# A recommender's lookups and layers: features transposed tile by tile, layers in blocks of two tiles, tables split by TensorE

## The chip, the cores and the metric

The kernel runs on one core of a Trainium2 chip. The metric is the device time of one execution in microseconds, the median of several runs. A profile is one execution recorded by the hardware's profiler, with all engines: TensorE (PE, its weight loads apart as PEld), VectorE (DVE), ScalarE (ACT), GpSimd (POOL) and the DMA queues.

## What is computed

For each of 16384 samples: 32 word rows of 300 floats are gathered from a table of 50000 rows and averaged; three bags of 20 rows of 64 floats are averaged from small tables (1000, 5000 and 10000 rows); four single rows come from tables of 100, 50, 20 and 1000 rows. The 748 features go through three layers. A scalar per looked-up row of the small tables (`wide`) is summed and added at the end.

```python
tok = word_emb[token_idx].mean(axis=1)            # 32 rows of 300
e1 = emb_mh1[mh1_idx].mean(axis=1)                # 20 rows of 64, and e2, e3 alike
o1 = emb_oh1[oh1_idx]                             # and o2, o3, o4
emb = jnp.concatenate([tok, e1, e2, e3, o1, o2, o3, o4], axis=1)   # 748
wide = (wide_mh1[mh1_idx].sum(axis=(1, 2)) + ... + wide_oh4[oh4_idx][:, 0])[:, None]
h = jax.nn.relu(emb @ W1 + b1)                    # 1024
h = jax.nn.relu(h @ W2 + b2)                      # 512
h = jax.nn.relu(h @ W3 + b3)                      # 256
return jax.nn.sigmoid(h @ Wd + bd + wide)
```

## The kernel before

A tile is 128 samples, and there are 128 tiles. Two things go on side by side.

The word rows are gathered by GpSimd: one indirect DMA per token position brings 128 rows of 1200 bytes, 32 of them per tile. VectorE adds them up.

```python
for q in range(n_groups):                          # 16 groups of two gathers
    rows = tokp.tile([P, TOK_GROUP * TOK_D], F32, name="tok_rows")     # 6 buffers
    for r in range(TOK_GROUP):
        nc.gpsimd.indirect_dma_start(
            out=rows[:, r * TOK_D : (r + 1) * TOK_D], out_offset=None, in_=word,
            in_offset=bass.IndirectOffsetOnAxis(ap=it[:, j : j + 1], axis=0))
    under_way.append((t, q, rows))
    if len(under_way) > TOK_LAG:                   # three groups later
        add_up(*under_way.pop(0))                  # two tensor_add on VectorE
```

The small tables are not gathered. Their rows lie on the chip, cut into 138 slices of 128 rows. VectorE makes one-hot rows for the slice number and for the row in the slice (`row`, `slice`), TensorE multiplies them into counts (`pc`), ScalarE copies the counts out (`cnt`, 8 bits), and TensorE multiplies the counts with the tables (`pg`). So that this is exact enough in 16 bits, each fp32 table is held as three bf16 terms, made once at the start:

```python
for part in range(n_h // PART):                    # six parts of 23 slices
    ...
    for c in range(3):
        if c:
            nc.vector.scalar_tensor_tensor(
                rows, rows, 2.0 if c == 1 else 1.0, term[c - 1], op0=ALU.mult, op1=ALU.subtract)
        nc.scalar.activation(term[c], rows, AF.Copy, scale=2.0 if c == 0 else 1.0)
        yield 1
```

The counts of a tile are made in 11 steps of 6 sample pairs. The program writes into each step the one-hots of the next step, this step's counts, some gathers, some of the last tile's sums, and some of the layers. The layers are fp32 and run over blocks of four tiles (512 columns), after a transpose of the block's features; the last tiles form blocks of two, one and one.

```python
def transposed(x, gs):                             # once per block of four tiles
    for k in range(NK):                            # six chunks of features
        pt = ps_h.tile([P, BLOCK], F32, name="pt", tag="ph")
        for s, g in enumerate(gs):
            nc.tensor.transpose(pt[:kk, s * P : (s + 1) * P], chunk(g, k), ident)
        nc.vector.tensor_scalar(x[:kk, k, 0:n], pt[:kk, 0:n], scale[:kk, k : k + 1], None, ALU.mult)
        yield CHUNK_WORK

def layer(dst, weights, bias, src, kks, n_out, n):
    for m in range(n_out):
        ph = ps_h.tile([P, BLOCK], F32, name="ph", tag="ph")           # two buffers in PSUM
        for k, kk in enumerate(kks):
            nc.tensor.matmul(ph[:, 0:n], weights[:kk, k, m * P : (m + 1) * P], src[:kk, k, 0:n],
                             start=(k == 0), stop=(k == len(kks) - 1))
            ...
        nc.scalar.activation(dst[:, m, 0:n], ph[:, 0:n], AF.Relu, bias=bias[:, m : m + 1])
```

The steps are put in order like this (cut):

```python
sizes = [NSUB] * (tiles // NSUB - 1) + [NSUB - 2, 1, 1]                # blocks of tiles
for t in range(tiles + 1):
    ...
    for i in range(STEPS):
        if t < tiles:
            hot = one_hots(sc, s, i + 1)
            counts(cnt, hot_now, i)
            tables_on_chip.to(TABLE_PACE * (t * STEPS + i - 2))
            toks.to(n_groups * (i + 1) / STEPS)
        done = next(sums) if sums else 0
        if layers:
            share = (n_h + layers_time) * (i + 1) / STEPS - done
            layers.to((layers_before + share) / LAYER_TIME)
    ...
    if len(gs) == sizes[0]:
        layers = Paced(mlp(b0, gs, wides))
```

Of the kernel before, what the change touches and what calls it, by code (L numbers as in the profile page):

```python
# [17 lines left out]
P = 128  # L18
# [5 lines left out]
TOK_LAG = 3  # L24
BLOCK = 512
HALF = P // 2
N_SMALL = 3 * N_MH + 4
ONEHOT = 6
STEPS = -(-HALF // ONEHOT)
CHUNK_WORK = 1  # L30
TABLE_PACE = 1.2
LAYER_TIME = 10
# [6 lines left out]
G_COLS = TOK_D + 7 * ROW  # L39
# [7 lines left out]
def kernel(  # L47
# [23 lines left out]
    NSUB = BLOCK // P  # L71
# [5 lines left out]
    for f in SMALL:  # L77
# [4 lines left out]
    tokp = ctx.enter_context(tc.tile_pool(name="tok", bufs=2 * TOK_LAG))  # L82
    const = ctx.enter_context(tc.tile_pool(name="const", bufs=1))
    idxp = ctx.enter_context(tc.tile_pool(name="idx", bufs=2))
# [4 lines left out]
    gp = ctx.enter_context(tc.tile_pool(name="g", bufs=NSUB + 1))  # L89
    wp = ctx.enter_context(tc.tile_pool(name="wide", bufs=2 * NSUB))  # L90
    xp = ctx.enter_context(tc.tile_pool(name="x", bufs=1))
# [8 lines left out]
        [(0, 128)],  # L100
        [(128, 256)],
        [(256, 300), (684, 748)],
        [(300, 428)],
        [(428, 556)],
        [(556, 684)],
    ]
# [7 lines left out]
    scale = const.tile([P, NK], F32, name="scale")  # L114
    nc.vector.memset(scale, 1.0)
    nc.vector.memset(scale[:, 0:2], 1.0 / N_TOK)
    nc.vector.memset(scale[0 : TOK_D - 256, 2:3], 1.0 / N_TOK)
    nc.vector.memset(scale[:, 3:4], 1.0 / N_MH)
    nc.vector.memset(scale[0:EMB, 4:5], 1.0 / N_MH)
# [23 lines left out]
    PART = n_h // 6  # L143

    def load_tables(part0, tag):
        raw = xp.tile([P, PART, ROW], F32, name="raw", tag=tag)
        for f in SMALL:
            table, (h0, h1) = tables[f], slices[f]
            full, rest = divmod(table.shape[0], P)
            a, b = max(h0, part0), min(h0 + full, part0 + PART)  # L150
            if a < b:
                nc.sync.dma_start(
                    out=raw[:, a - part0 : b - part0, :],
                    in_=table[(a - h0) * P : (b - h0) * P, :].rearrange("(h p) d -> p h d", p=P),
                )
            if rest and part0 <= h0 + full < part0 + PART:
                nc.vector.memset(raw[:, h0 + full - part0, :], 0.0)
                nc.sync.dma_start(out=raw[0:rest, h0 + full - part0, :], in_=table[full * P :, :])
        return raw

    def convert_tables():
# [3 lines left out]
        raws = [load_tables(k * PART, tags[k]) for k in range(2)]  # L165
        yield
        for part in range(n_h // PART):
            rows = raws[part]
            if 1 <= part < n_h // PART - 1:
                raws.append(load_tables((part + 1) * PART, tags[(part + 1) % 2]))  # L170
            for c in range(3):
                term = [
                    terms[:, part * PART : (part + 1) * PART, k * ROW : (k + 1) * ROW]
                    for k in range(3)
                ]
                if c:
                    nc.vector.scalar_tensor_tensor(
                        rows, rows, 2.0 if c == 1 else 1.0, term[c - 1], op0=ALU.mult, op1=ALU.subtract
                    )
                nc.scalar.activation(term[c], rows, AF.Copy, scale=2.0 if c == 0 else 1.0)  # L180
                yield 1
# [22 lines left out]
    under_way = []  # L204
    features = {}

    def add_up(t, q, rows):
# [4 lines left out]
        else:  # L212
            nc.vector.tensor_add(tok_sum, tok_sum, a)  # L213
            to = features[t][:, 0:TOK_D] if q == n_groups - 1 else tok_sum
            nc.vector.tensor_add(to, tok_sum, b)  # L215

    def tokens(t, it):


        for q in range(n_groups):  # L220
            rows = tokp.tile([P, TOK_GROUP * TOK_D], F32, name="tok_rows")
            for r in range(TOK_GROUP):
                j = q * TOK_GROUP + r
                nc.gpsimd.indirect_dma_start(  # L224
                    out=rows[:, r * TOK_D : (r + 1) * TOK_D],
                    out_offset=None,
                    in_=word,
                    in_offset=bass.IndirectOffsetOnAxis(ap=it[:, j : j + 1], axis=0),
                )
            under_way.append((t, q, rows))  # L230
            if len(under_way) > TOK_LAG:
                add_up(*under_way.pop(0))
            yield 1

    def last_tokens():
        for group in under_way:
            add_up(*group)

    def load_indices(blk):
# [15 lines left out]
        return it, ix  # L255
# [71 lines left out]
    def small_sums(g, cnt):  # L327
# [3 lines left out]
        for i in (0, 2, 4, 6):  # L331
# [9 lines left out]
            at = TOK_D + i * ROW  # L341
# [9 lines left out]
    def wide_term(g):  # L351
        wide = wp.tile([P, 1], F32, name="wide")
        at = TOK_D + EMB
        nc.vector.tensor_reduce(
            wide,
            g[:, at : at + 6 * ROW].rearrange("p (c d) -> p c d", d=2 * ROW)[:, :, 0:2],
# [3 lines left out]
        nc.vector.tensor_add(wide, wide, g[:, G_COLS - 1 : G_COLS])  # L360
        return wide

    def chunk(g, k):
        if k < 2:
            return g[:, k * P : (k + 1) * P]
        if k == 2:
            return g[:, 2 * P : TOK_D + EMB]
        at = TOK_D + (1 + 2 * (k - 3)) * ROW + 1
        return g[:, at : at + 2 * EMB]

    def transposed(x, gs):

        n = len(gs) * P
        for k in range(NK):
            kk = chunk_k[k]
            pt = ps_h.tile([P, BLOCK], F32, name="pt", tag="ph")
            for s, g in enumerate(gs):
                nc.tensor.transpose(pt[:kk, s * P : (s + 1) * P], chunk(g, k), ident)  # L378
            nc.vector.tensor_scalar(  # L379
                x[:kk, k, 0:n], pt[:kk, 0:n], scale[:kk, k : k + 1], None, ALU.mult  # L380
            )
            yield CHUNK_WORK

    def layer(dst, weights, bias, src, kks, n_out, n):
        for m in range(n_out):
            ph = ps_h.tile([P, BLOCK], F32, name="ph", tag="ph")
            for k, kk in enumerate(kks):
                nc.tensor.matmul(  # L388
                    ph[:, 0:n],
                    weights[:kk, k, m * P : (m + 1) * P],  # L390
                    src[:kk, k, 0:n],
                    start=(k == 0),
                    stop=(k == len(kks) - 1),
                )
                if k < len(kks) - 1:
                    yield 1
            nc.scalar.activation(dst[:, m, 0:n], ph[:, 0:n], AF.Relu, bias=bias[:, m : m + 1])  # L397
            yield 1

    def mlp(b0, gs, wides):  # L400

        n = len(wides) * P
        x = xp.tile([P, NK, BLOCK], F32, name="x", tag="even")
        yield from transposed(x, gs)
        h1 = xp.tile([P, M1, BLOCK], F32, name="h1", tag="odd")
        yield from layer(h1, w1_sb, b1_sb, x, chunk_k, M1, n)
        h2 = xp.tile([P, M2, BLOCK], F32, name="h2", tag="even")
        yield from layer(h2, w2_sb, b2_sb, h1, [P] * M1, M2, n)
        h3 = xp.tile([P, M3 + 1, BLOCK], F32, name="h3", tag="odd")
        yield from layer(h3, w3_sb, b3_sb, h2, [P] * M2, M3, n)  # L410
        po = ps_h.tile([1, BLOCK], F32, name="po", tag="ph")
        for k in range(M3):
            nc.tensor.matmul(  # L413
                po[:, 0:n], wd_sb[:, k : k + 1], h3[:, k, 0:n], start=(k == 0), stop=False
            )
        for s, wide in enumerate(wides):
            nc.tensor.matmul(  # L417
                po[:, s * P : (s + 1) * P], wide, ident, start=False, stop=(s == len(wides) - 1)
            )
        y = h3[0:1, M3, 0:n]  # L420
        nc.scalar.activation(y, po[:, 0:n], AF.Sigmoid, bias=bd_sb)
# [3 lines left out]
    class Paced:  # L425


        def __init__(self, gen):
            self.gen, self.done = gen, 0

        def to(self, size):
            while self.done < size:
                work = next(self.gen, None)
                if work is None:
                    return
                self.done += work
# [27 lines left out]

    tiles = B // P
    mlp_time = (NK * (CHUNK_WORK + M1) + M1 * M2 + M2 * M3 + M3) * LAYER_TIME
    ctx.enter_context(tc.manual_schedule())
    sizes = [NSUB] * (tiles // NSUB - 1) + [NSUB - 2, 1, 1]
    it, ix = load_indices(0)
# [5 lines left out]
    gs, wides, layers, before, b0 = [], [], None, None, 0  # L475
    for t in range(tiles + 1):
        s = t % NSUB
        sums = None
        if before:
            features[t - 1] = g = gp.tile([P, G_COLS], F32, name="g")  # L480
            sums = sums_by_step(small_sums(g, before))
        if t < tiles:
            if s == 0 and t:
                it, sc = next_it, next_sc
            cnt = cp.tile([P, 2, HALF, n_h], FP8, name="cnt", tag="counts")
            toks = Paced(tokens(t, it[:, s, :].bitcast(U32)))
        else:
            last_tokens()
        for i in range(STEPS):
            if t < tiles:  # L490
                hot_now = hot
                if s == 1 and i == 0 and t + NSUB < tiles:
                    next_it, ix = load_indices(t // NSUB + 1)
                if s == 2 and i == 0 and t + NSUB < tiles + 1:
                    next_keys = lookup_keys(ix)
                if i < STEPS - 1:
                    hot = one_hots(sc, s, i + 1)
                elif t + 1 < tiles:
                    hot = one_hots(next_sc if s == NSUB - 1 else sc, (s + 1) % NSUB, 0)
# [65 lines left out]
```

## Time and profile before

| what | value |
|---|---|
| time, median of 3 runs | 7126.95 us (7116.23 to 7129.94) |
| span of the profiled execution | 5269.3 us |
| mean granted TensorE clock in it | 0.989 |
| gathers (GpSimd) | 4096, 951 ns each |
| TensorE matmuls in the record | 41320 |
| layer matmuls in the record (two per fp32 matmul) | 5984, busy 1474.1 + 1211.0 us |
| sums from the tables, `pg` | 17664, busy 1849.6 us |
| counts, `pc` | 16384, busy 758.4 us |
| one-hots on VectorE | 2816, busy 762.4 + 797.9 us |
| token adds on VectorE | 3968, 479 ns each |
| HBM traffic | 123 GB/s |

The profiled execution is shorter than the measured ones; the table gives both. In the lines of the profile, a group of instructions stands with its count, its busy time, the mean length of one, and the idle time of its engine before it with what ended that idle time. Matmuls overlap in a pipeline, so the mean length of one is longer than the busy time divided by the count. A weight load (PEld) runs beside the matmul ahead of it.

### The profile page before, as it was taken

How to read it: one execution, taken by the hardware profiler on the slowest of the kernel's cores; microseconds unless marked ns; L12 is line 12 of the kernel's file. 1: busy time of each engine (PE TensorE's matmuls, PEld its weight loads, DVE VectorE, ACT ScalarE, POOL GpSimd, SP SyncE). 2: the span in 40 equal slices, each digit the busy share in tenths (PEclk: the TensorE clock that was granted, in tenths of full speed). 3: DMA queues.
4: the chain of work that ended last, by engine and by line, in shares of the span. 5: the costliest groups of instructions: out<-in, count | busy, mean ns of one | idle time of the engine just before them, and what ended most of it. 6: DMA issues, size and time to landing. Idle time of an engine off the chain costs nothing.

```text
span 5269.3 us, 104252 instructions
## 1 busy us (share of the span) xinstructions
PE 5094.7 (97%) x41320; PEld 3164.7 (60%) x41320; DVE 3768.8 (72%) x8014; ACT 2447.1 (46%) x1938; POOL 3897.3 (74%) x4103
## 2 busy tenths in 40 slices
PE   4799999999999999999999999999999999999999
PEld 3565656566565656656655656556566566656658
DVE  8777777777777777777777777777777777777752
ACT  5444444444444444444444444444444444444432
POOL 7777777777777777777777777777777777777762
PEclk8899999999999999999999999999999999999999
DMA  6444444444444444444444444444444444444431
GB/s 190 125 125 124 125 125 126 126 125 124 125 125 125 125 124 125 125 125 126 125 124 125 126 125 126 124 125 125 125 125 125 124 126 125 125 125 125 124 103 34
DMA packets 252890, 652.60 MB, mean 124 GB/s; under 512 B 119009, under 2 KB 119524, under 8 KB 252399
## 3 DMA queue, kind: packets, MB, share of 16 engines
q0 software_dynamic: 196608, 629.41, 43.5%
q1 hardware_dynamic: 55791, 16.53, 1.4%
q8 instruction: 323, 5.29, 0.4%
q14 instruction: 168, 1.38, 0.1%
HBM read 645.59 MB, written 0.07 MB: 123 GB/s over the span
## 4 chain that ended last, share of the span: by engine, by line
PE 37%; DMA 23%; DVE 16%; issue 14%; POOL 10%; ACT 0%; DVEq 0%; SPq 0%; POOLq 0%; ACTq 0%
DMA tok_rows<-in_word_emb_dram,it 22%; PE ph L388 20%; PE pg L337 12%; POOL tok_rows L224 10%; DVE own L215 5%; PE pc L312 4%; DVE own L213 3%; DVE slice L294 3%; DVE row L294 2%; DVE x L379 1%; DVE g L343 1%; PE po L413 1%; DVE own L211 0%; DVE g L215 0%; PE po L417 0%
## 5 line engine op out<-in xcount | busy, mean ns | idle before, releaser
L224 POOL DMA_INDIRECT tok_rows<-in_word_emb_dram,it x4096 | 3896.4, 951 | 1293.4 <-issue 755.5
L319 ACT ACTIVATE cnt<-pc 128x1656 fp8e3<-128x1656 f32 (+1 forms) x1408 | 2121.7, 1507 | 2056.4 <-PE pc L312 2026.0
L337 PE MATMUL pg<-terms,cnt 128*128 128x195 bf16 x17664 | 1849.6, 254 | 87.7 <-DVE g L343 86.3
L337 PEld LDWEIGHTS <-cnt 128*128 128x128 fp8e3 x17664 | 1601.3, 144 | 234.6 <-issue 81.1
L388 PE MATMUL ph<-x,w_sb 128*128 128x512 f32 (+5 forms) x3264 | 1474.1, 581 | 4.2 <-DVE x L379 3.5
L215 DVE TENSOR_TENSOR own<-own,tok_rows 128x300 f32<-128x300 f32 x1792 | 857.7, 479 | 680.6 <-DMA tok_rows<-in_word_emb_dram,it 647.3
L388 PE MATMUL ph<-h,w_sb 128*128 128x512 f32 (+2 forms) x2720 | 1211.0, 573 | 0.0
L213 DVE TENSOR_TENSOR own<-own,tok_rows 128x300 f32<-128x300 f32 x1920 | 918.8, 479 | 387.6 <-DMA tok_rows<-in_word_emb_dram,it 335.8
L312 PEld LDWEIGHTS <-row 64*128 64x128 bf16 x16384 | 501.7, 95 | 1041.3 <-DVE own L215 246.1
L294 DVE TENSOR_TENSOR row<-own,sc 128x768 bf16<-128x768 bf16 (+1 forms) x1408 | 762.4, 541 | 162.8 <-PE pc L312 89.5
L312 PE MATMUL pc<-slice,row 64*128 64x138 bf16 x16384 | 758.4, 224 | 70.6 <-DVE slice L294 36.7
L388 PEld LDWEIGHTS ph<-x,w_sb 128*128 128x128 f32 (+1 forms) x3264 | 564.3, 194 | 414.6 <-issue 401.9
L294 DVE TENSOR_TENSOR slice<-own,sc 128x828 bf16<-128x828 bf16 (+1 forms) x1408 | 797.9, 567 | 0.0
L388 PEld LDWEIGHTS ph<-h,w_sb 128*128 128x128 f32 x2720 | 463.3, 192 | 317.9 <-issue 316.0
L397 ACT ACTIVATE h<-ph,b_sb 128x512 f32<-128x512 f32 (+2 forms) x476 | 316.3, 665 | 683.2 <-PE ph L388 678.2
L343 DVE TENSOR_REDUCE g<-pg 128x130 f32<-128x390 f32 (+1 forms) x512 | 259.2, 506 | 151.1 <-PE pg L337 150.8
L379 DVE TENSOR_SCALAR x<-pt,scale 128x512 f32<-128x512 f32 (+4 forms) x204 | 137.0, 712 | 3.7 <-PE pt L378 2.9
L378 PE MATMUL pt<-ident,g 128*128 128x128 f32 (+1 forms) x768 | 104.1, 275 | 3.0 <-DVE x L379 2.5
L211 DVE TENSOR_TENSOR own<-tok_rows 128x300 f32<-128x300 f32 x128 | 61.4, 480 | 49.5 <-DMA tok_rows<-in_word_emb_dram,it 47.3
L378 PEld LDWEIGHTS pt<-ident,g 128*128 128x128 f32 (+1 forms) x768 | 85.5, 141 | 7.7 <-DVE x L379 6.7
L215 DVE TENSOR_TENSOR g<-own,tok_rows 128x300 f32<-128x300 f32 x128 | 60.2, 471 | 22.3 <-DMA tok_rows<-in_word_emb_dram,it 18.3
L413 PE MATMUL po<-h,wd_sb 128*1 128x512 f32 (+2 forms) x136 | 60.9, 566 | 0.3
(34 smaller groups left out, 290.1 us busy)
## 6 DMA issues: line engine op xcount, KB each, us to landing
tok_rows<-in_word_emb_dram,it POOLq DMA_INDIRECT x4096
ix<-in_idx_dram SPq DMA_DIRECT2D x128, 32.0 KB
w_sb<-in_W_dram SPq DMA_DIRECT2D x6, 512.0 KB
raw<-in_mh_dram SPq DMA_DIRECT2D x3, 747.5 KB
it<-in_idx_dram SPq DMA_DIRECT2D x32, 64.0 KB
w_sb<-in_W_dram SPq DMA_DIRECT2D x1, 2048.0 KB
raw<-in_mh_dram SPq DMA_DIRECT2D x1, 617.5 KB
out_dram<-h SPq DMA_DIRECT2D x31, 2.0 KB
```

The lines of the kernel that those rows point to most:

```text
L213: nc.vector.tensor_add(tok_sum, tok_sum, a)
L215: nc.vector.tensor_add(to, tok_sum, b)
L224: nc.gpsimd.indirect_dma_start(out=rows[:, r * TOK_D : (r + 1) * TOK_D], out_offset=None, in_=word, in_offset=bass.IndirectOffsetOnAxis(ap ...
L294: nc.vector.tensor_tensor(one[:, 0:rows, :].rearrange("p i (n d) -> p i n d", d=2), iota[:, 0:n].rearrange("p (n d) -> p n d", d=2).unsque ...
L312: nc.tensor.matmul(pc[:, f, k // n, at : at + n_h], hot[0][half, k, :], hot[1][half, k, :], start=True, stop=True,)
L319: nc.scalar.activation(cnt[:, :, b : b + rows, :].rearrange("l f (g k) h -> l f g (k h)", g=2), pc[:, :, :, 0 : n * n_h], AF.Copy, scale=0 ...
L337: nc.tensor.matmul(pg[:, j, :], by_slice[:, :, h], terms[:, h, :], start=(h == h0), stop=(h == h1 - 1))
L343: nc.vector.tensor_reduce(g[:, at : at + n * ROW].rearrange("p (f d) -> p f d", f=n), pg[:, 0:n, :].rearrange("p f (c d) -> p f d c", c=3) ...
L378: nc.tensor.transpose(pt[:kk, s * P : (s + 1) * P], chunk(g, k), ident)
L379: nc.vector.tensor_scalar(x[:kk, k, 0:n], pt[:kk, 0:n], scale[:kk, k : k + 1], None, ALU.mult)
L388: nc.tensor.matmul(ph[:, 0:n], weights[:kk, k, m * P : (m + 1) * P], src[:kk, k, 0:n], start=(k == 0), stop=(k == len(kks) - 1),)
L397: nc.scalar.activation(dst[:, m, 0:n], ph[:, 0:n], AF.Relu, bias=bias[:, m : m + 1])
```

## The change

The features no longer wait for a block of four tiles. Each tile's small features are transposed once its sums are done, and its token features once its rows are added up, in two groups of transposes per tile. The layers run over blocks of two tiles (256 columns). The sum of the wide terms rides along in the transpose and is added by VectorE at the end in place of matmuls with the identity. The token rows no longer keep step with their tile: all groups are spread evenly over all steps and 16 more, so they drift behind the counts over the course of the execution; eight row buffers take the place of six. The splitting of the tables into terms moves from VectorE to TensorE: the remainder is a matmul with twice the identity, less matmuls of the earlier terms with minus the identity. The purpose is to begin the layers earlier, to leave less for the end, and to free VectorE at the start.

```diff
 TOK_LAG = 3
+TOK_BUFS = 8
+WAKE = 16
 BLOCK = 512
+LAYER_TILES = 2
 ...
-    PART = n_h // 6
+    twice = const.tile([P, P], F32, name="twice")
+    minus = const.tile([P, P], BF16, name="minus")
 ...
-                if c:
-                    nc.vector.scalar_tensor_tensor(
-                        rows, rows, 2.0 if c == 1 else 1.0, term[c - 1], op0=ALU.mult, op1=ALU.subtract
-                    )
-                nc.scalar.activation(term[c], rows, AF.Copy, scale=2.0 if c == 0 else 1.0)
+            left = ps_h.tile([P, SPLIT, ROW], F32, name="left", tag="ph")[:, 0 : b - a, :]
+            nc.tensor.matmul(left, twice, rows(p), start=True, stop=False)
+            for k in range(c):
+                nc.tensor.matmul(left, minus, term(p, k), start=False, stop=(k == c - 1))
+            nc.scalar.activation(term(p, c), left, AF.Copy)
 ...
-    def transposed(x, gs):
 ...
+        def add_small(self, t, g):
+            at = self.columns(t)
+            pt = ps_h.tile([P, 4, P], F32, name="pt", tag="ph")
+            nc.tensor.transpose(pt[:, 3, :], g[:, 0:P], ident)
+            for k in range(3):
+                c = (1 + 2 * k) * ROW + 1
+                nc.tensor.transpose(pt[:, k, :], g[:, c : c + P], ident)
+            nc.vector.tensor_tensor(
+                self.small[:, 0:3, at], pt[:, 0:3, :], scale.unsqueeze(2).to_broadcast([P, 3, P]), ALU.mult
+            )
+            nc.vector.tensor_copy(self.small[0:EMB, 3, at], pt[0:EMB, 3, :])
+            nc.vector.tensor_copy(self.wide[:, at], pt[EMB : EMB + 1, 3, :])
+
+        def add_tokens(self, t, g):
 ...
+            pt = ps_h.tile([P, 3, P], F32, name="pt", tag="ph")
+            for k in range(2):
+                nc.tensor.transpose(pt[:, k, :], g[:, k * P : (k + 1) * P], ident)
+            nc.tensor.transpose(pt[0 : EMB + rest, 2, :], g[:, TOK_D - rest - EMB : TOK_D], ident)
+            nc.vector.tensor_single_scalar(self.tok[:, :, at], pt[:, 0:2, :], 1.0 / N_TOK, op=ALU.mult)
+            nc.vector.tensor_single_scalar(
+                self.small[EMB : EMB + rest, 3, at], pt[EMB : EMB + rest, 2, :], 1.0 / N_TOK, op=ALU.mult
+            )
 ...
-        for s, wide in enumerate(wides):
-            nc.tensor.matmul(
-                po[:, s * P : (s + 1) * P], wide, ident, start=False, stop=(s == len(wides) - 1)
-            )
 ...
+        nc.vector.tensor_add(y, po[:, 0:n], block.wide[:, 0:n])
+        nc.scalar.activation(y, y, AF.Sigmoid, bias=bd_sb)
 ...
+    n_steps = tiles * STEPS + WAKE
+    sizes = [LAYER_TILES] * (tiles // LAYER_TILES - 1) + [1] * LAYER_TILES
 ...
+        if waiting and step >= waiting[0][0]:
+            block = transpose(*waiting.pop(0)[1:])
+            if block:
+                if layers:
+                    layers.finish()
+                layers = Paced(mlp(block), LAYER_TIME * block.n / P)
 ...
+        toks.to(n_all * (step + 1) / n_steps)
```

## The prediction

> **What bounds the kernel now.** I read the page of the profile first (busy time by engine), then the gathers' own row, then short pieces of the timeline, and last the first and the last stretches of the execution. The page names TensorE:
>
> ```profile
> PE 5094.7 (97%) x41320; PEld 3164.7 (60%) x41320; DVE 3768.8 (72%) x8014; ACT 2447.1 (46%) x1938; POOL 3897.3 (74%) x4103
> ...
> L224 POOL DMA_INDIRECT tok_rows<-in_word_emb_dram,it x4096 | 3896.4, 951 | 1293.4 <-issue 755.5
> ```
>
> POOL at 74% looks far from the bound, but its idle time is not free time. This is the middle of the execution, POOL alone (start, length, what; in brackets the idle time before it):
>
> ```profile
> 3001.23 0.95 POOL L224 DMA_INDIRECT tok_rows<-in_word_emb_dram,it  x1 [0.30 <-issue]
> 3002.48 0.95 POOL L224 DMA_INDIRECT tok_rows<-in_word_emb_dram,it  x1 [0.30 <-DVE own L215]
> 3003.74 0.94 POOL L224 DMA_INDIRECT tok_rows<-in_word_emb_dram,it  x1 [0.30 <-issue]
> ```
>
> Every gather takes 0.95 us and 0.30 us pass before the next, whatever the row says ended the gap. So the pace of a gather is 1.25 us, and a tile of 128 samples (32 gathers) cannot be shorter than 32 x 1.25 = 40.0 us. The same row over the stretch from 94 to 5000 us:
>
> ```profile
> L224 POOL DMA_INDIRECT tok_rows<-in_word_emb_dram,it x3914 | 3713.0, 949 | 1193.5 <-issue 718.1 <-DVE own L215 291.5 <-DVE own L213 63.4
> ```
>
> 3914 gathers in 4906 us is 1.2535 us each: POOL runs at its own pace for 93% of the execution. TensorE is tuned to fit just under it: 5094.7 / 128 = 39.8 us of busy time per tile against 40.1 us. So the kernel has two bounds a fraction of a microsecond apart, and what lies above 4096 x 1.25 = 5120 us is at the two ends. The end, by stretches (busy us of PE, PEld, DVE, ACT, POOL):
>
> ```profile
> 4750.00:5000.00 250.00, 248.46 (x2020) 151.82 (x2015) 180.66 (x382) 118.29 (x93) 189.31 (x200) 1.00 0.46 125
> 5025.00:5190.00 165.00, 163.17 (x1096) 102.67 (x1094) 83.73 (x173) 60.47 (x55) 92.43 (x98) 1.00 0.34 92
> 5190.00:5269.00 79.00, 75.07 (x631) 67.61 (x629) 13.05 (x35) 17.98 (x39) 1.02 (x2) 1.00 0.02 5
> ```
>
> Up to 5000 us there are 200 gathers in 250 us. Then TensorE must push the layers of a block of four tiles through two tiles' time, and the gathers fall behind: the 118 between 5000 and 5190 us would need 148 us at their pace, so about 40 us are lost. After the last gather (5190 us) TensorE works alone for 79 us. At the start, the first 64 gathers end at 94 us, against 3 + 64 x 1.25 = 83 us: 11 us lost. Three of the lines there:
>
> ```profile
> 22.07 1.50 POOL L224 DMA_INDIRECT tok_rows<-in_word_emb_dram,it  x1 [0.30 <-issue]
> ...
> 24.72 1.71 DVE L177 SCALAR_TENSOR_TENSOR raw<-raw,terms 128x1495 f32<-128x1495 f32 x1
> ...
> 25.16 2.09 POOL L224 DMA_INDIRECT tok_rows<-in_word_emb_dram,it  x1 [0.30 <-issue]
> ```
>
> A gather issued beside the table-splitting VectorE instruction took 2.09 us instead of 0.95.
>
> **The time and the profile differ.** The measured time is 7127 us, the profiled execution 5269 us. Nothing in the profile says what the other 1858 us are. Three readings are possible: gathers that are slower ((7127 - 82) / 4096 = 1.72 us each), a TensorE that is slower throughout, or a cost per TensorE instruction that the profiled execution doesn't have. I carry over differences in microseconds, not the bound.
>
> [...] The trace has both widths, because the last blocks of before are short:
>
> ```profile
> L388 PE MATMUL ph<-h,w_sb 128*128 128x512 f32 x2480 | 1173.9, 598 | 0.0
> ...
> L388 PE MATMUL ph<-h,w_sb 128*128 128x256 f32 x80 | 18.2, 380 | 0.0
> ```
>
> Busy by count: 473 ns at 512 columns and 228 ns at 256, so two halves (456 ns) are no dearer than one whole, although each has its own weight load.
>
> **The change, part by part.** The order of instructions built from both kernels gives the counts.
>
> Gathers: 4096 before and after, unchanged, with eight buffers of two rows in place of six and the sums spread over 1424 steps instead of 1408. The floor stays 4096 x 1.25 us.
>
> Layers in blocks of two tiles: 2992 fp32 matmuls become 5720, each half as wide. By the 473 and 228 ns above: 0 us, at most +13 us.
>
> Transposes: 6 per tile (768) become 7 (896). At 104.1 / 768 = 136 ns each that is +17 us. The wide term's 128 matmuls go (33.5 us on the page of forms): -33 us. But the transposes now come in two groups per tile, between count matmuls and sums, and each group takes one of the two PSUM buffers of the layers. The order shows the next layer group waiting for VectorE's copy out of it. Per group I estimate 0.1 to 0.5 us of TensorE wait (a copy of 128x256 took 0.48 us before): 256 x 0.1 to 0.5 = +25 to +130 us of TensorE time.
>
> VectorE: six scalings of 743 ns per four tiles (1.1 us per tile) become five small operations per tile. By the scalings of the short blocks (0.35 us at 128 columns, 0.48 at 256, 0.74 at 512) I estimate 0.6 + 0.48 + 3 x 0.35 = 2.1 us; one microsecond more in 40 is hidden at 72% busy, unless it falls between two one-hots.
>
> Table splitting: the 12 VectorE instructions of 1.71 us go; about 100 identity matmuls replace them while TensorE is half idle (first 130 us: 63 us busy). This gives back the 11 us of late gathers.
>
> The end: all counts, small sums and layers but those of the last tile are done when the last gather lands. What remains is 2.9 us from issue to landing (the chain near the end has such pieces), two sums (0.95 us), transposes and copies (1 us), one tile's layers (19.97 us for 176 matmuls in the chain of before), two activations and the store (3 us): 28 us in place of 79, so -51 us. The four-tile squeeze of the layers goes too: up to -40 us.
>
> Sum for a gather-bound execution: -11 - 51 - 40 = -102 us in the profile if TensorE still fits. It hardly does: 39.8 us per tile plus 0.1 to 0.9 us against 40.0. So I expect some 30 to 60 us of the 102 back: the profile at about 5210 us. In the timed execution, if gathers are 1.72 us apart, a tile has 55 us, TensorE fits with ease, and the squeeze (60 us per tile before) cost only some 10 us: -11 - 10 - 51 = -72 us. 7127 - 72 = 7055; I say 7050 us.
>
> **Rivals.** (1) TensorE becomes the bound: if the timed execution has a slow TensorE (39.8 x 7127 / 5269 = 54 us per tile), the tail's gain shrinks, as work only moves, and the added waits count in full: 7080 to 7250 us. For it: PE busy 97%. Against: the gathers' even 1.25 us from the start, when TensorE has no layers to do. (2) A cost per TensorE instruction: matmul records grow by some 14% (5984 of 41320 double), so up to 8100 us. Against: in the trace 176 matmuls with their loads pass in 19.97 us, 57 ns an instruction, so no such cost is visible; I give it 5%. (3) The landing of rows, not their issue, is the timed bound; then eight buffers instead of six could bring much more, down to 6500 us or less. For it: VectorE waits 1001 us for landings. Against: those waits end in step with POOL's own pace, and DMA is 46% busy. I give it 7%. (4) The transposes' wait falls on VectorE's one-hot chain, so that each tile loses 1 us: 7180 us.
>
> **Range and chances.** The middle is a gain of 50 to 100 us, 1%. Rival 1 and 4 put the upper end at 7190, rival 3 and the full 102 us scaled by 7127 / 5269 (138 us) the lower at 6940. Faster than 6984 us: 0.20; within 2%: 0.67; slower than 7270: 0.13.
>
> **What would show it.** In the profile of the changed kernel: gathers still 1.25 us apart in the middle; the first 64 issued by 84 us and none of 2 us; about 28 us between the last gather and the end; 228 to 244 ns per 256-column matmul; TensorE waits on VectorE's copies under 60 us in all. It is wrong if the middle has more than 41 us per tile (TensorE took over), if layer matmuls cost over 250 ns each, or if the profile changes by one amount and the time by another of a different size.

## The result, and the profile after

| kernel | time, median | range |
|---|---|---|
| before | 7122.07 us (4 runs) | 7116.23 to 7129.94 |
| changed | 7677.58 us (4 runs) | 7650.32 to 7694.15 |

The changed kernel is slower: ratio 1.0775, 95% interval 1.0738 to 1.0813. That is 555 us more, against 77 us less in the prediction.

The profile of the front (5269 us) could not be set beside it, because it is of other circumstances than the times: in six series of runs the kernel before took 7122 to 7137 us, in two others 5261 and 5273 us (one chip gave both), and nothing in the kernel decides which. So the kernel before was profiled once more where it takes 7130.31 us. Three lines of that page, the kernel before: busy time by engine, then two groups (busy, mean ns of one, idle time of the engine before it and what ended most of it):

```profile
PE 5683.3 (80%) x41320; PEld 3488.7 (49%) x41320; DVE 3796.8 (53%) x8014; ACT 2465.7 (35%) x1938; POOL 3882.1 (54%) x4103
...
L224 POOL DMA_INDIRECT tok_rows<-in_word_emb_dram,it x4096 | 3881.2, 948 | 3167.9 <-DVE own L215 1650.1
...
L294 DVE TENSOR_TENSOR row<-own,sc 128x768 bf16<-128x768 bf16 (+1 forms) x1408 | 761.8, 541 | 2006.0 <-remote 1451.8
```

The same lines of the page of the changed kernel:

```profile
PE 5997.8 (78%) x46912; PEld 4709.9 (61%) x46912; DVE 3889.4 (51%) x8503; ACT 2577.0 (34%) x2445; POOL 3877.2 (50%) x4103
...
L256 POOL DMA_INDIRECT tok_rows<-in_word_emb_dram,it x4096 | 3876.3, 946 | 3771.4 <-DVE own L244 2456.7
...
L323 DVE TENSOR_TENSOR row<-own,sc 128x768 bf16<-128x768 bf16 (+1 forms) x1408 | 762.3, 541 | 1864.1 <-remote 1424.9
```

A gather takes 0.95 us as ever. But no engine is near 100% any more, in neither kernel. GpSimd waits 1650 us (before) and 2457 us (changed) for VectorE's adds to free row buffers, and VectorE waits over 1400 us, ahead of its one-hots, for "remote": a signal whose sender the trace does not show. What this is, a stretch of the timeline of the changed kernel tells (start, length, what; in brackets the idle time before):

```profile
4004.09 1.03 PE L443 MATMUL ph<-x_tok,w_sb 128*128 128x256 f32 x4
...
4005.49 0.54 PE L341 MATMUL pc<-slice,row 64*128 64x138 bf16 x12
...
4010.69 0.32 PE L366 MATMUL pg<-terms,cnt 128*128 128x195 bf16 x1 [0.24 <-issue]
...
4011.43 0.32 PE L366 MATMUL pg<-terms,cnt 128*128 128x195 bf16 x1 [0.41 <-issue]
...
4015.04 0.47 ACT L452 ACTIVATE h<-ph,b_sb 128x256 f32<-128x256 f32 x1 [10.73 <-remote]
...
4015.14 0.56 DVE L323 TENSOR_TENSOR row<-own,sc 128x768 bf16<-128x768 bf16 x1 [8.53 <-remote]
...
4015.41 1.54 ACT L348 ACTIVATE cnt<-pc 128x1656 fp8e3<-128x1656 f32 x1
```

The counts (`pc`) are done by 4006.0 us, yet VectorE's next one-hot and ScalarE's copy of the counts, which wait for them, start at 4015.1 and 4015.4. In between TensorE begins one or two `pg` matmuls about every 0.7 us and stands in "issue", that is, it waits for nothing that the trace shows. I call this a hold: for some 10 us TensorE gets on at a fraction of its rate, and what waits for its finished counts starts late. The same stretch by windows (length, busy us and count of PE, PEld, DVE, ACT, POOL, then TensorE's granted clock, DMA share and GB/s):

```profile
4002.00:4006.00 4.00, 4.00 (x48) 3.28 (x43) 3.72 (x8) 1.55 (x1) 3.09 (x4) 1.00 0.63 159
4006.00:4015.00 9.00, 3.72 (x17) 1.75 (x16) 0.57 (x2) 0.00 (x0) 5.19 (x6) 0.70 0.42 117
4015.00:4020.00 5.00, 5.00 (x25) 3.60 (x25) 2.42 (x5) 2.33 (x3) 1.89 (x2) 0.51 0.11 32
```

GpSimd alone, same kernel, same place:

```profile
4000.53 0.94 POOL L256 DMA_INDIRECT tok_rows<-in_word_emb_dram,it  x1 [8.77 <-DVE own L244]
4001.78 0.95 POOL L256 DMA_INDIRECT tok_rows<-in_word_emb_dram,it  x1 [0.30 <-issue]
...
4011.77 0.95 POOL L256 DMA_INDIRECT tok_rows<-in_word_emb_dram,it  x1 [0.30 <-issue]
4017.49 0.94 POOL L256 DMA_INDIRECT tok_rows<-in_word_emb_dram,it  x1 [4.77 <-DVE own L244]
```

GpSimd goes on gathering every 1.25 us and then waits until VectorE, freed at 4015, adds and so frees a row buffer. So a hold shows at the gathers as a gap. Counted over the trace, from one gather's start to the next: in the kernel before 475 gaps of over 3 us, 2249 us together; in the changed kernel 562, 3113 us together (in the profile of the front, which has no holds, 13 and 54 us). Outside of the gaps the pace is 1.25 us in both. The last gather starts at 7049.6 us before and at 7648.2 us after, +599; the end behind it shrinks from 78.9 to 39.8 us. So the loss lies ahead of the last gather, and the gaps of over 3 us alone grow by 864 us (the shorter intervals, 87 fewer of them, give back 266). In TensorE's terms, of 560 us more, 315 are busy time and 245 idle time.

The end of the changed kernel, in the same form:

```profile
7648.00:7688.00 40.00, 36.97 (x317) 35.06 (x316) 9.49 (x24) 9.61 (x26) 0.94 (x1) 1.00 0.03 9
```

And the start: the gathers near 25 us, where one took 2.09 us, are even now. One of them:

```profile
24.43 0.95 POOL L256 DMA_INDIRECT tok_rows<-in_word_emb_dram,it  x1 [0.30 <-issue]
```

### The profile page after: what moved, and what is told of

Read it like the earlier page. It is cut to its first block, busy times and chain, and to the rows that moved or that the text cites. A ratio compares the mean times of both kernels' runs of the same rounds, so it can differ in the third digit from the quotient of the medians.

```text
span 7688.0 us, 116518 instructions
## 1 busy us (share of the span) xinstructions
PE 5997.8 (78%) x46912; PEld 4709.9 (61%) x46912; DVE 3889.4 (51%) x8503; ACT 2577.0 (34%) x2445; POOL 3877.2 (50%) x4103
## 4 chain that ended last, share of the span: by engine, by line
PE 51%; another core or an unknown queue 20%; DVE 13%; issue 11%; ACT 5%; DVEq 0%; SPq 0%; DMA 0%; ACTq 0%
PE ph L443 23%; PE pg L366 17%; PE pc L341 8%; DVE own L240 4%; ACT cnt L348 4%; DVE slice L323 3%; DVE own L244 3%; DVE row L323 1%; PE po L468 1%; PE pt L411 1%; ACT h L452 1%; PE pt L427 1%; DVE g L372 1%; PE pt L408 0%
## 5 line engine op out<-in xcount | busy, mean ns | idle before, releaser
L366 PE MATMUL pg<-terms,cnt 128*128 128x195 bf16 x17664 | 2184.0, 273 | 475.6 <-issue 422.4
L366 PEld LDWEIGHTS <-cnt 128*128 128x128 fp8e3 x17664 | 1805.8, 147 | 738.5 <-issue 617.7
L443 PE MATMUL ph<-h,w_sb 128*128 128x256 f32 (+1 forms) x5200 | 1387.5, 410 | 81.4 <-issue 77.9
L443 PE MATMUL ph<-x_small,w_sb 128*128 128x256 f32 (+3 forms) x4160 | 1204.1, 417 | 78.2 <-issue 61.1
L443 PEld LDWEIGHTS ph<-h,w_sb 128*128 128x128 f32 x5200 | 1021.6, 210 | 260.9 <-issue 133.9
L452 ACT ACTIVATE h<-ph,b_sb 128x256 f32<-128x256 f32 (+1 forms) x910 | 426.7, 469 | 1830.2 <-remote 879.8
L443 PEld LDWEIGHTS ph<-x_small,w_sb 128*128 128x128 f32 (+1 forms) x4160 | 824.2, 212 | 233.7 <-issue 121.6
L443 PE MATMUL ph<-x_tok,w_sb 128*128 128x256 f32 (+1 forms) x2080 | 626.7, 408 | 19.7 <-issue 19.0
L443 PEld LDWEIGHTS ph<-x_tok,w_sb 128*128 128x128 f32 x2080 | 411.9, 210 | 87.9 <-issue 35.8
L468 PE MATMUL po<-h,wd_sb 128*1 128x256 f32 (+1 forms) x260 | 88.7, 467 | 41.8 <-ACT h L452 30.6
```

Of the source, the lines that this page charges most:

```text
L366: nc.tensor.matmul(pg[:, j, :], by_slice[:, :, h], terms[:, h, :], start=(h == h0), stop=(h == h1 - 1))
L443: nc.tensor.matmul(ph[:, 0:n], weights[: src.shape[0], k, m * P : (m + 1) * P], src, start=(k == 0), stop=(k == len(srcs) - 1),)
L468: nc.tensor.matmul(po[:, 0:n], wd_sb[:, k : k + 1], h3[:, k, 0:n], start=(k == 0), stop=(k == M3 - 1))
```

## The experiments

Each was run beside the kernel before; "before" is its median in that series. In the expectations, A with a number stands for theories in which TensorE itself is the cause (A2: the multiplying), B for gathers that are slower one by one; the later letters are explained where they come. "Gaps" are starts of gathers more than 3 us apart, counted in the profiled execution of each run.

**e0: the kernel before, unchanged.** For a profile that belongs to the measured time.

> The kernel before, unchanged, for a profile that belongs to its measured time. The profile of 5269 us on hand and the measured 7122 us differ by 1853 us. Theory A (TensorE stalls): about 7120 us, with TensorE stretches of several us in which its instructions come 0.35 us apart, some 1800 us in all, and a mean granted clock of about 0.88, as in the changed kernel's profile. Theory B (gathers slower): 1.72 us between gathers everywhere and TensorE's stream as clean as in the profile of 5269 us.

Measured: 7130.31 us. Its lines stand above. The gathers are not slower one by one: four of five intervals between their starts are still 1.25 us. B, the first of my three readings in the prediction, falls.

**e1: the kernel before with halved layer matmuls.** Blocks of four tiles stay, but each fp32 matmul of 512 columns becomes two of 256: 5984 more matmuls and as many weight loads in the record, the same multiplying.

```diff
-            for k, kk in enumerate(kks):
-                nc.tensor.matmul(ph[:, 0:n], weights[...], src[:kk, k, 0:n], ...)
+            for at in (0, n // 2):
+                for k, kk in enumerate(kks):
+                    nc.tensor.matmul(ph[:, at : at + n // 2], weights[...], src[:kk, k, at : at + n // 2], ...)
```

> The kernel before, with each layer matmul done as two matmuls of half as many columns (blocks of four tiles kept, all else kept). TensorE multiplies the same columns, but has 14% more instructions. Theory A1 (stalls come with the number of TensorE instructions): 7122 us + 300 to 600 us, near the 7677 us of the changed kernel. Theory A2 (stalls come with the multiplying itself[...]): within 1% of 7122 us. Theory A3 (the changed kernel lost its time to the waits of its two transposes per tile): within 1% of 7122 us as well.

Measured: 7465.73 us, before 7136.78; ratio 1.0446 (1.0418 to 1.0474), +329 us, or 55 ns for each added matmul; 552 gaps. That is 59% of what the change loses, but not all of it lies where the change loses it. In the profiled execution (7487 us) 154.4 us pass behind the last gather, against 78.9 in e0. The edit halves the last single tiles as well, from 128 to 64 columns, and there two halves cost nearly twice one whole (start, length, what); and the last tile runs at half of the clock (a window, in the form above):

```profile
7344.28 3.54 PE L389 MATMUL ph<-h,w_sb 128*128 128x128 f32 x30
...
7386.28 3.93 PE L389 MATMUL ph<-h,w_sb 128*128 128x64 f32 x34
...
7410.00:7480.00 70.00, 70.00 (x330) 70.00 (x329) 0.00 (x0) 4.77 (x13) 0.00 (x0) 0.50 0.00 0
```

The changed kernel has neither: its layers have no matmul of 64 columns, and its end is 39.8 us. Ahead of the last gather the halving costs 282 us in this execution (47 ns for each added matmul) and the whole change 599. So this single part makes about half of the loss there.

**e2: the changed kernel with layers over half the columns.** Half of the layers' multiplying is left out, the number of matmuls stays; the activations write both halves from the one half.

```diff
-                    ph[:, 0:n], weights[...], src,
+                    ph[:, 0 : n // 2], weights[...], src[:, 0 : n // 2],
```

> The changed kernel with the same number of layer matmuls and weight loads, but each over half of its columns (half of the layers' work is left out; ScalarE copies each half result twice). Theory A1 (instructions count): 7400 to 7700 us. Theory A2 (columns multiplied[...]): 1270 us of multiplying go, so 6000 to 6500 us, and the granted clock rises.

Measured: 7673.32 us, before 7136.78; ratio 1.075 (1.0721 to 1.0779). TensorE is busy for 5236 us in place of 5998, and the time is that of the changed kernel, though the mean granted clock is lower too, 0.783 against 0.877. What the layers multiply is not what is waited for; how many instructions they are may be.

**e3: the changed kernel with blocks of three tiles.** 3780 fewer matmul records; six row buffers, and two buffers each for the small features and the wide rows, to make room.

```diff
-TOK_BUFS = 8
+TOK_BUFS = 6
-LAYER_TILES = 2
+LAYER_TILES = 3
```

> The changed kernel with blocks of three tiles (384 columns) in place of two, six row buffers in place of eight, and two buffers for the small features and wide rows so that it fits. 7392 fewer TensorE instructions, everything else of the change kept. Theory A1 (TensorE instructions cost 28 ns each, as the halved layers of the kernel before showed): 7677 - 207 = 7470 us, and what then still lies above 7130 us is not the count. Theory A3 (the waits of the two transposes per tile): the same number of transposes, so about 7650 us.

Measured: 7589.59 us, before 7129.9; ratio 1.0658 (1.0632 to 1.0683), 88 us less than the changed kernel. The direction of e1, at about half its rate: 23 ns per matmul here, 47 to 55 ns there.

**e4: the kernel before with a quarter of the gathers.** Only every fourth group is gathered, and its rows are added four times; three quarters of the gathers are left out, all else stays.

```diff
+            if q % 4 == 0:
+                rows = tokp.tile([P, TOK_GROUP * TOK_D], F32, name="tok_rows")
-            for r in range(TOK_GROUP):
+            for r in range(TOK_GROUP if q % 4 == 0 else 0):
```

> The kernel before with only every fourth group of word rows gathered and used four times (three quarters of the gathers are left out; all adds stay). Theory D (the gathers' traffic or GpSimd's work holds TensorE up): the stalls shrink to a quarter, about 5600 us. Theory A1 (TensorE's own instructions bring the stalls): 7050 to 7150 us.

Measured: 5156.82 us, before 7129.9; ratio 0.7238 (0.7217 to 0.7259). From its page, busy time by engine and the one-hots:

```profile
PE 5060.7 (98%) x41320; PEld 3144.5 (61%) x41320; DVE 3795.2 (74%) x8014; ACT 2444.0 (47%) x1938; POOL 969.5 (19%) x1031
...
L295 DVE TENSOR_TENSOR row<-own,sc 128x768 bf16<-128x768 bf16 (+1 forms) x1408 | 761.0, 540 | 654.5 <-PE pc L313 622.4
```

TensorE has all its 41320 matmuls and is 98% busy; the wait for "remote" is gone. The holds come with the gathers.

**e5: the kernel before with half of the sums.** Every second `pg` matmul is left out: 8576 fewer matmuls in the record.

```diff
-                    nc.tensor.matmul(pg[:, j, :], ..., stop=(h == h1 - 1))
+                    if (h - h0) % 2 == 0:
+                        nc.tensor.matmul(pg[:, j, :], ..., stop=(h >= h1 - 2))
```

> The kernel before with every second matmul of the sums from the tables left out, 17152 TensorE instructions fewer of 82640, and 750 us less of multiplying. If TensorE's instructions pass at a capped rate (11.6 per us over the whole execution): 65488 / 11.6 = 5650 us. If each instruction costs 28 ns on top: 7130 - 480 = 6650 us. If the stalls had nothing to do with them, the gathers' floor of 1.25 us each plus the stalls: about 7000 us.

Measured: 7069.68 us, before 7129.9; ratio 0.9925 (0.9902 to 0.9948): 60 us less. A plain charge per TensorE instruction would have given 8576 x 55 = 470 us by the rate of e1, and some 400 by its 47 ns. So there is none; the layers' instructions weigh more than those of the sums. Why, no run shows.

**e6, e7, e8: the row buffers.** Theory E came from the timeline: a hold seems to end some 3 us after the last gather that finds a buffer, so more buffers might make longer holds.

```diff
-    tokp = ctx.enter_context(tc.tile_pool(name="tok", bufs=2 * TOK_LAG))
+    tokp = ctx.enter_context(tc.tile_pool(name="tok", bufs=7))        # e6; bufs=4 in e8
...
-TOK_BUFS = 8
+TOK_BUFS = 6                                                           # e7, in the changed kernel
```

> The kernel before, with seven buffers for the token rows in place of six, nothing else. Theory E (while gathers flow TensorE is held back, and it recovers only once GpSimd runs out of row buffers; so every buffer more makes each hold longer): 50 to 120 us slower than before, 7180 to 7250 us, about 450 holds of 10.5 to 11.5 us. Theory F (the holds come from the gathers, but how long GpSimd may run ahead does not matter): 7110 to 7145 us. The row buffers as a help (the third rival of the prediction): under 7080 us.

> The changed kernel with six buffers for the token rows in place of eight, nothing else. Theory E: 100 to 230 us faster than the changed kernel, 7450 to 7580 us; so the buffers are much of what the change costs beyond its more numerous layer instructions. Theory F: 7640 to 7700 us as before.

> The kernel before with four buffers for the token rows in place of six. Theory E: shorter holds, 100 to 300 us faster than before, 6830 to 7030 us, unless GpSimd then stands without need between the holds. Theory F: no gain; 7130 us, or up to 300 us slower because a gather then waits for VectorE's add more often.

Measured: seven buffers 7143.57 us, ratio 1.0009 (0.9996 to 1.0022); four buffers 7142.1 us, 1.0007 (0.9997 to 1.0018); the changed kernel with six 7686.36 us, 1.076 (1.071 to 1.0811), all beside 7136.74. Theory E falls, F holds. How far GpSimd may run ahead has no part in it.

**e9: the kernel before with a pause after each gather.**

```diff
+    pause = const.tile([P, 384], F32, name="pause")
...
                     in_offset=bass.IndirectOffsetOnAxis(ap=it[:, j : j + 1], axis=0),
                 )
+                nc.gpsimd.memset(pause, 0.0)
```

> The kernel before with a GpSimd memset of 128x384 after every gather, which takes some 0.4 us, so that gathers can be no closer than about 1.65 us and 4096 of them need 6760 us. Theory E, or any theory in which it is the dense stream of gathers that holds TensorE back: the holds become few, the time is 6800 to 6950 us, faster than before though GpSimd has more to do. If the holds depend on the number of gathers alone: 450 holds of 10 us as before, 7130 to 7400 us.

Measured: 6503.8 us, before 7136.74; ratio 0.9103 (0.9082 to 0.9124). GpSimd does 1784 us more work, and the kernel is 633 us faster. Its page:

```profile
PE 5411.1 (83%) x41320; PEld 3328.1 (51%) x41320; DVE 3773.8 (58%) x8014; ACT 2452.0 (38%) x1938; POOL 5709.3 (88%) x8199
...
L225 POOL DMA_INDIRECT tok_rows<-in_word_emb_dram,it x4096 | 3934.3, 961 | 712.1 <-issue 556.2
...
L231 POOL MEMSET pause<- 128x384 f32 x4096 | 1784.1, 436 | 2.7
...
L296 DVE TENSOR_TENSOR row<-own,sc 128x768 bf16<-128x768 bf16 (+1 forms) x1408 | 761.4, 541 | 130.6 <-PE pc L314 31.0
```

The gathers start every 1.55 us, GpSimd no longer waits for VectorE's adds, and the one-hots' idle time is 131 us in place of 2006. Five gaps are left of 475. A tile takes about 50 us from the first to the last: GpSimd's own pace is the bound.

**e10, e11, e12: a shorter pause, and the changed kernel with both.**

```diff
+    pause = const.tile([P, 160], F32, name="pause")                    # e10 (before), e12 (changed)
+    pause = const.tile([P, 384], F32, name="pause")                    # e11 (changed)
...
+                nc.gpsimd.memset(pause, 0.0)
```

> The kernel before with a shorter memset (128x160, some 0.23 us) after every gather, so a gather every 1.35 us and a floor of 5530 us. Theory G (the holds are a matter of how dense the gathers follow each other, with a limit between 1.25 and 1.55 us): if 1.35 is above the limit, 5600 to 5800 us; if below it, holds as before, 7000 to 7150 us. Theory H (TensorE is slowed in proportion to the rate of gathers, and the mean rate settles near one in 1.6 to 1.7 us whatever is done): 6500 to 6900 us.

> The changed kernel with the memset of 128x384 (0.44 us) after every gather. If what the change costs comes by way of the holds: it is as short as the gathers' pace allows, and the shorter end counts, 6440 to 6490 us, 0.2 to 1% faster than the kernel before with the same memset (6503.8). If its more numerous TensorE instructions and waits cost by themselves: 6600 to 7000 us.

> The changed kernel with the memset of 128x160 after every gather. Theory G with 1.35 us above the limit: 5560 to 5800 us; below it: 7550 to 7700 us. Theory H: 6600 to 7200 us, and slower than the kernel before with the same memset by 2 to 7%, as its TensorE has more to issue.

Measured, all beside a before of 7125.01 us:

| pace of gathers | kernel before, gaps | changed kernel, gaps |
|---|---|---|
| 1.25 us, no pause | 7122.07 us, 475 | 7677.58 us, 562 |
| 1.36 us, 160 columns | 6873.08 us, 327 | 7229.42 us, 413 |
| 1.55 us, 384 columns | 6503.8 us, 5 | 6442.3 us, 0 |

The ratios to before are 0.9637 (0.9593 to 0.9681) for e10, 0.9036 (0.9008 to 0.9063) for e11, 1.0127 (1.0091 to 1.0163) for e12. The sparser the gathers, the fewer holds; at 1.36 us they are thinned out, at 1.55 us gone. That is nearer to H (a slowing in proportion) than to G (a sharp limit): e10 lies in the range of H, e12 29 us above it and 5.2% above e10. The changed kernel loses 555, then 356 us, and where the holds are gone it gains 61.5 (e9 and e11 are of two series, whose kernels before are 12 us apart). The page of e11:

```profile
PE 5437.4 (84%) x46912; PEld 4413.0 (69%) x46912; DVE 3850.7 (60%) x8503; ACT 2608.5 (41%) x2445; POOL 5710.7 (89%) x8199
...
L257 POOL DMA_INDIRECT tok_rows<-in_word_emb_dram,it x4096 | 3934.0, 960 | 698.0 <-issue 550.8
...
L325 DVE TENSOR_TENSOR row<-own,sc 128x768 bf16<-128x768 bf16 (+1 forms) x1408 | 762.1, 541 | 81.1 <-PE pc L343 6.4
```

One may object that TensorE has slack here, which could hide a cost of its own. But its busy time is 5437 against 5411 us in e9, +26, where the unpaced pair differs by 315; and its idle time in "issue" is 4 against 10 us, where the unpaced pair has 662 and 376. The cost itself is absent, not hidden.

**e13, e16: short rows.** Rows of 400 bytes in place of 1200; the table is read as three times as many rows, the adds take each third three times. Two thirds of the bytes are left out.

```diff
-                    out=rows[:, r * TOK_D : (r + 1) * TOK_D],
+                    out=rows[:, r * TOK_D : r * TOK_D + 100],
-                    in_=word,
+                    in_=word.rearrange("n (k d) -> (n k) d", k=3),
```

> The kernel before, in which every gather brings 128 rows of 400 bytes in place of 1200 (the table seen as three times as many rows of 100 floats; two thirds of each row are left out, and the adds read the third three times). The number of gathers, their pace on GpSimd and all else stay. If it is the bytes that hold TensorE back: the holds vanish, 5250 to 5500 us. If it is the number of gathers[...]: holds as before, 6950 to 7150 us.

> The same as e13: the kernel before with rows of 400 bytes in place of 1200 (two thirds of each row left out), once more, because in the job of e13 the kernel before itself took 5261 us, without the holds, so that nothing could be told. If the kernel before takes some 7130 us beside it: bytes as the cause give 5250 to 5500 us, the number of gathers 6950 to 7150 us. If the kernel before takes 5261 us again: 5252 us again.

Measured: e13 5252.14 us beside a before of 5261.33, a series in which nothing holds, so that it tells nothing of the question. e16: 7110.16 us, before 7134.05; ratio 0.9968 (0.9954 to 0.9982). The one-hots in e16:

```profile
L297 DVE TENSOR_TENSOR row<-own,sc 128x768 bf16<-128x768 bf16 (+1 forms) x1408 | 762.8, 542 | 1979.4 <-remote 1426.2
```

The same wait as with full rows, with 233 MB moved in place of 653; 479 gaps. So the bytes are not what matters. The number of gathers, each still of 128 rows, does not make the holds by itself either, as e9 has all 4096 of them: it is how densely they follow each other.

**e14, e15, e17: the changed kernel with pauses of 288 and 336 columns.** The edit is that of e11 with these widths.

> The changed kernel with a memset of 128x288 after every gather (0.36 us by the 0.25 us of 160 columns and the 0.44 us of 384), a gather every 1.47 us, floor 6060 us. By the two points there are (1.55 us: no holds left, 6442; 1.36 us: 413 holds, 7229) in proportion: 6550 to 6900 us. If the holds have a limit just under 1.55 us: the same; if one well below: 6080 to 6200 us.

> The changed kernel with a memset of 128x336 (0.40 us), a gather every 1.51 us, floor 6230 us. In proportion: 6400 to 6650 us; if the limit is below 1.5 us: 6250 to 6300 us.

> The same as e14: the changed kernel with a memset of 128x288 after every gather, a gather every 1.47 us, once more beside a kernel before that has the holds (7130 us). If the limit of the holds lies below 1.47 us: 6085 to 6150 us, and the best time of all under these circumstances. If the holds grow in proportion between 1.55 us (none) and 1.36 us (413, 7229 us): 6550 to 6900 us. If the kernel before takes 5261 us: 6087 us again.

Measured: e14 6087.11 us and e15 6260.95 us beside a before of 5261.33; e17 6101.14 us beside 5272.8 (ratio 1.1571, 1.155 to 1.1591). Again series without holds, so where they cease between 1.36 and 1.55 us stays open. What they show is the price of the pause where it isn't needed: e14 is 4096 x 1.473 = 6033 us of gathers and the two ends, 16% slower than the kernel before. The paced versions beat both kernels only where the holds are: e11, 6442.3 us, is the fastest measured there.

## Why the prediction was wrong

**The step that failed** is the bridge from the profile to the time: "I carry over differences in microseconds, not the bound." The 1858 us were not a constant on top. They were made by holds, and the change makes more of these: 562 gaps in place of 475. With it fell the dismissal of the second rival: "so no such cost is visible; I give it 5%." True of that trace, but the trace was of an execution without the 1858 us; what they consist of could not be seen in it. A difference of 1858 us that I could not name was larger than every effect I weighed, and a range of 250 us and a chance of 0.13 for slower took no account of it.

By its terms:

- *Gathers 1.25 us apart in the middle.* Right outside of the gaps, and no bound here: the kernel before takes 2000 us more than 4096 x 1.25. One of the prediction's signs of being wrong, "more than 41 us per tile", is there: 32 gathers take 59.7 us (median) in the changed kernel, but 55.0 us in e0 already.
- *"Layers in blocks of two tiles ... 0 us, at most +13 us."* Right for the multiplying, wrong for this execution. Where nothing holds, two halves cost one whole: the page by forms has 521 ns of busy time per 512-column matmul in e9,

```profile
L390 PE MATMUL ph<-h,w_sb 128*128 128x512 f32 x2480 | 1291.7, 650 | 0.0
```

  and 260 ns per 256-column one in e11:

```profile
L445 PE MATMUL ph<-h,w_sb 128*128 128x256 f32 x5040 | 1309.3, 406 | 13.3 <-DVE x_small L432 12.0 <-DVE sc L311 1.3
```

  From 512 to 256 columns the traces show no extra cost; from 128 to 64 they do (e1: 118 and 116 ns each). Both means in e9 and e11 are above the 473 and 228 ns of the prediction, with a granted clock of 0.935 and 0.945 in place of 0.989. Beside dense gathers the same halving cost 329 us, 282 of the profiled execution's ahead of the last gather (e1). This was the term that was mis-sized.
- *Waits of the transposes, +25 to +130 us of TensorE.* At the top of the range: in e11 TensorE's idle time ahead of transposes is 8 us, that for `x_small` 54 and that for `wide_row` 67 us. The prediction's sign for waits on VectorE's copies, "under 60 us in all", did not come true. In e11 GpSimd's pace hides them.
- *The start, -11 us.* Right where it can be seen: the 64th gather starts at 101.2 us in e11, at 113.1 us in e9. In the changed kernel itself the gathers are even at first, but holds then delay the 64th to 120.9 us (101.6 in e0).
- *The squeeze, -10 us.* -1 us: the last gather comes 13 us earlier in e11 than in e9, 12 of them from the start.
- *The end, 28 us in place of 79.* 29.2 us in e11, and 39.8 us in the changed kernel.
- Start and end, -11 and -51 us, are what the change is worth once nothing holds: -61.5 us measured between e9 and e11, against -72 predicted with the squeeze.

**The rivals.** (2) was the nearest: the time grew with the number of TensorE instructions (e1, e3), but not at a fixed charge (e5: 7 ns per matmul, e1: 47 to 55). (1) fails, TensorE is 78% busy, and half its layers' work may go without a gain (e2). (3) fails: four, six or seven buffers are the same (e6, e8), eight or six in the changed kernel too (e7). (4), a slower one-hot chain by the transposes, is not seen: in e11 the one-hots wait 81 us in all, less than in e9.

One more rival is the granted clock, 0.901 in e0 and 0.877 in the changed kernel, against 0.989 in the profile of the front. It falls in the course of a hold and not ahead of it: in the stretch shown from 1.00 to 0.70 and 0.51, and over the 236 waits for "remote" of more than 5 us on VectorE of the changed kernel from 0.97 (10 to 8 us before such a wait ends) to 0.62 (2 to 4 us after). And in e1's last 70 us shown, at 0.50, TensorE works without a pause. So the lower clock goes with longer matmuls behind a hold (six of 256 columns in 2.82 us from 4015.07 us, 470 ns each, at 0.50; four in 1.03 us from 4004.09 us, 258 ns each, at 1.00), but does not start one.

**What stays open.** Shown: the loss is made in holds, which need dense gathers, do not depend on their bytes or on row buffers, and grow with the layers' instructions. Ahead of the last gather the halving alone makes 282 of 599 us (e1); the other half was not taken apart. Between e1 and the changed kernel, with nearly equal numbers of matmuls, lie the 128 transposes more, two groups of them per tile, and ScalarE's 910 activations of the layers in place of 476. What in a gather reaches TensorE was not found, nor why two series were free of it, nor how the changed kernel without pauses runs in such a series. Each time on record has a span and a granted clock of its own beside it, so all are of recorded executions; whether one that is not recorded has holds is open too.

## What to carry to other kernels

If the profile is a quarter shorter than the measured times, it isn't a profile of them: take one whose span matches the time before any term of it is carried over, and don't treat the difference as a constant. Look for "remote" and "issue" waits beside an engine that had long been done, and for gaps on the DMA-issuing engine. Where GpSimd issues gathers back to back and such waits fill the trace, a short pause behind each may gain more than it costs; measure it in more than one series, as nothing here shows a gain from it where nothing holds: with pauses the changed kernel is 16% slower there than the kernel before without them.

## What the runs showed of the hardware

- Halving an fp32 matmul's columns was free from 512 to 256 (521 ns of busy time each in e9, 260 in e11), but not from 128 to 64: 30 in 3.54 us and 34 in 3.93 us, 118 and 116 ns each (e1).
- More work on GpSimd made a kernel faster: 4096 memsets of 0.44 us, 1784 us in all, for 633 us less (e9).
- Beside dense gathers TensorE's issue slows in spells of some 10 us in these runs (in the changed kernel 15 `pg` matmuls take 9.3 us from 4005.96 us, where 15 took 1.52 us at 4002.28 us), and other engines' waits for its results end late (the one-hot's after 8.53 us, at 4015.14 us), while the gathers themselves go on at 1.25 us. In the profile of the front gathers as dense do not do this: 13 gaps in place of 475.
- The trace's record of semaphore changes differs as well. Each of the eight semaphores of the gathers tells of 512 of them. In the profile of the front 8151 to 8177 separate changes are recorded for each, 15.9 to 16.0 for a gather; in e0 2128 to 3881, in the changed kernel 2257 to 3647, in e9 3539 to 5420. Why there are fewer was not shown. This goes with the series and not with the holds: e11, without a gap, has 4209 to 4569, and e14, the same kernel with a shorter pause in a series without holds, 8180 to 8192. Whether the holds belong to the recording or to the kernel was not shown either.
